# A hand-ordered four-layer graph kernel: a block sum written in place, six sum buffers, three attention tiles, eleven halves of x

## The chip, the core and the metric

The kernel runs on one core of a Trainium2 chip. A core has TensorE (PE in the profile: matmuls and transposes), VectorE (DVE), ScalarE (ACT), GpSimd (POOL) and SyncE (SP, which here issues the DMAs). Each works through its own queue in order and waits for others by semaphores. The time is the device time of one execution in microseconds, and less is better.

## The reference

The input x has 128 graphs of 128 nodes with 512 features, in fp32. All graphs share one 128x128 adjacency matrix. Four layers follow each other, each with a residual and a layer norm. The kernel receives all of them, and the second adds a per-row amount that the following layer norm takes away again, so that only its second normalisation is left of it (the kernel folds this into a factor of the first).

```python
# layer 0: x = LN(x + norm_adj @ (x @ W0) + bias), with norm_adj = D^-1/2 adj D^-1/2
# layer 1: x = LN(x + max over a row of relu(pre)), with the adjacency for both weights
# layer 2
q, k, v = x @ Wq.T, x @ Wk.T, x @ Wv.T
rel = adj.T * (q @ k.T)
x = LN(x + (rel / norm(rel, axis=2)) @ v)
# layer 3
h = x @ W3
e = leaky_relu(s1[:, None] + s2[None, :]) * adj      # s1 = h @ a1, s2 = h @ a2
x = LN(x + elu(softmax(e) @ h + beta * h))
```

## The kernel before

**Groups and steps.** Four graphs make a group, and there are 32 groups, 0 to 31. A group is a chain of 240 steps for the repeated part. Some of their names, in the order of one group's chain:

- `ld` loads a half of x (two graphs, 512 KB); `y` is norm_adj times x, transposed; `cy` copies it to SBUF; `bi` adds the bias to x on POOL.
- `w1` to `w7` are the seven products of one level of Strassen's scheme for y times W0; `dw` adds them onto x; `stw`, `gw`, `pow`, `apw` are layer norm statistics, guard, power and application.
- `xt` and `xd` transpose x: blocks of 32x32 on DVE (`xt`), and an exchange by 16 DMAs of 64 KB on SP (`xd`, line 680). The result is the tile that the profile calls x_<group>T.
- `z1` to `z7` and `v1` to `v7` are products of that transpose, with Wq and Wk folded into one weight `gq`, and with Wv. `c` copies or `d` adds bring them into C_z and C_v. `r` multiplies z with x (line 1142, tile pr), `rm`, `sq`, `rp` mask it and take its norm, `rt`, `wr`, `cr` transpose it through DRAM (relT), `f` multiplies it with v (line 1190, tile pl_v), and `fa` adds it onto x with a running total (line 1199).
- `mnv`, `qv`, `gv`, `pov`, `apv` normalise: negative mean and squares on ACT, the power on POOL (line 588), the application on ACT (line 1029).
- `nt` and `nd` transpose x once more (tile n_<group>T), again with 16 DMAs; `k1` to `k7` multiply it with W3 into C_k.
- `sc` are the two attention scores of a graph on DVE (line 1214); `pw` and `pe` send one of them through DRAM and back to all partitions; `pl`, `ej`, `ei`, `ex`, `rd`, `so` are leaky relu, mask, maximum, exponential and division; `at`, `aw`, `cat` transpose the result through DRAM (attT); `h` multiplies it with C_k (line 1190, tile pl_k); `em`, `ee`, `ea` finish the elu; `mnk`, `qk`, `gk`, `pok`, `apk` normalise, and `fin` stores.

**Two levels of Strassen.** A left side (y, x or n transposed) is a class `Left` with a tile of four blocks, `block(p, h)`, over halves of the graphs and halves of the features. `sum(0)` to `sum(3)` (steps `sy`, `sx`, `sn`) make its four sums on POOL; products 5, 6, 7 and 3 read them through `of`. `sum(i)` computes them in the order sum 0, 2, 1, 3; the one made second is `A(0,0) - A(1,0)`, read by product 7. Products 1, 2, 5 (for z and v also 4) are split once more: `l12`, `l5`, `l4` (method `small`) make POOL sums of 128x128 blocks; the first four small matmuls are the step `w1` (line 730), the further three have a name such as `w18`, and between them the steps `b` (ACT copies a part out of PSUM) and `e` (three DVE additions). Products that are not split have four matmuls of 256 columns (line 766).

**The order.** Each instruction's place in its engine's queue follows from three written strings. `HEAD` starts the first groups, `TURN` is repeated and moves every stage on by one group, and `TAIL` ends. A step is written as group.step, the group counted from the turn's base; text below uses true group numbers, as in 31.f1. Before, `TURN` is used 14 times. `BACK`, `FIRST` and `LAST` set which groups it spans. Group 31 has steps of its own (class attribute `HALVES`): it transposes its attention matrices on PE (prt, pat, ps2) in place of the way through DRAM, and its last products k and h are split into halves of the columns for one or two graphs.

**Buffers.** `Slotted.tile` takes the slot of a shared buffer from the strings of `SLOTS`, one character an allocation: `bank` (PSUM), `S` (the sums, 2 KB a partition, seven of them), `m` (attention tiles such as rel, ru, relT, e, s2, au, attT, 2 KB, four), `x` (halves of x, 4 KB, ten), `aT` (transposes, three) and others. A new tile in a slot waits for the last reader of the one before.

Of the kernel before, what the change touches and what calls it, by code (L numbers as in the profile page):

```python
# [37 lines left out]
F32 = mybir.dt.float32  # L38
# [10 lines left out]
        "012345012345013324015345231455124240510435012532245312312023543413421402402052145230142402"  # L49
        "405233100340153013205320521340135305355234252351453524503210430454115310512125312305211451"  # L50
        "412523102304253042541105305015021541030340351405232432352315320142424230314525325435403451"
        "025252541243050250302310324152525234530121521015041053425252503201454254142134120352525210"
        "514323523435403451025252541243050250302310324152525234530121521015041053425252503201454254"
        "142134120352525210514323523435403451025252541243050250302310324152525234530121521015041053"
        "425252503201454254142134120352525210514323523435403451025252541243050250302310324152525234"
        "530121521015041053425252503043201513105140152035033042453510140541524513202020314220445020"
        "545523405212550033235143024014515313210213142055015354151041043201425125523020130023054354"
        "2045151501250312315415401340132145131523152403145324501324051324051"
    ),
    "S": (  # L60
        "012345601326054321502461532143250123654012106425231064104632501462035142560413524651203546"
        "413406524103561463205164231534062135410216534012605403216504352651403256124320651423046145"
        "320641563062145360231534062135410216534012605403216504352651403256124320651423046145320641"
        "563062145360231534062135410216534012631450326154036413652014326504152602324316052432560324"
        "152630645016325064152306"
    ),
    "l1": (
        "010111010101010010101011001101001011010010110100101101001011010010110100101101001011010010"
        "110100110010110011010110100100110"
    ),  # L70
    "l2": (
        "010101010101010010110110110110110110110110110110110110110110110110110110110110110101110101"
        "01"
    ),
    "C": (
        "010101010101011010101011011011011011011011011011011011011011011011011011011011011011011010"
        "10101010"
    ),
    "aT": (
        "012100212102102012012102012102012102012102012102012102012102012102012102012102102012012010"  # L80
        "2110210"
    ),
    "m": (
        "012301202302301210320100130133212013131201310310213231201012103232120131323021213103232120"
        "131323021213103232120131323021213103232120131323021213103232120131323021213103232120131323"
        "02121310233221302022132020213201210312121203210030"
    ),
    "x": (
        "0123457869789012345768901234576890123457689012345768901234576981032"
    ),  # L90
    "q": (
        "010101010101010001001010101010101010101010101011010101010101010100101010101001010101010101"
        "010101010101010001010101010101010101010101010101010101010101010101010101010101010101010101"
        "010101010101010101010101010101010101010101010101010101010101010101010101010101010101010101"
        "010101010101010101010101010101010101010101010101010101010100010101010101010101010101010101"
        "01010101010101010101010101010101010101010101010101010101010101010101010"
# [3 lines left out]
MIDS = 4  # L100
SUMS = 7
# [5 lines left out]
LAST = -7  # L107
# [3 lines left out]
0.ld1 2.ld0 0.ld0 2.ld1 1.ld1 1.ld0 s.warm s.deg s.root s.nadj s.adjt s.nadjT 0.y10 0.y01 0.cy10  # L111
1.y10 0.cy01 1.y11 1.cy10 1.y01 1.cy11 0.y11 s.m012_0 1.cy01 3.ld1 s.s00 0.w2 s.m012_1 0.cy11
s.s02 0.bi10 s.m012_3 0.y00 0.bi01 2.y10 s.s01 0.cy00 2.y11 0.bi00 0.w1 s.m05_0 0.sy0 s.s03 2.y00
1.y00 0.bi11 s.m05_1 1.cy00 0.sy2 s.m012_2 0.w5 1.bi10 s.m05_3 0.sy3 0.dw1 s.m05_2 0.w6 0.sy1
0.dw2 s.sk0 1.ly12 s.sk2 s.g1 0.dw6 s.s30 0.w7 s.cg1 1.sy0 s.m312_0 1.bi11 0.dw7 s.m312_1 0.w4
1.bi00 0.dw5 s.bi 0.w3 s.sa1 2.cy10 0.dw4 2.cy00 s.sk1 2.cy11 s.g2 s.sa0 0.dw3 0.stw3 3.y11 1.bi01
0.stw0 s.g5 0.stw1 s.sa2 s.dg2 2.y01 s.s31 1.sy2 0.stw2 1.w2 2.cy01 s.s33 s.g6 0.gw s.sa3 1.bw2
s.m35_0 1.w1 s.cg6 0.pow 1.ew2 s.g7 1.bw1 s.m35_1 2.bi11 1.ew1 0.apw0 0.apw1 1.w28 0.xt0 1.ly5
1.w18 s.cg7 s.sk3 s.la 0.apw2 0.apw3 1.sy1 1.w5 1.dw1 3.ld0 0.xt2 s.g4 1.bw5 0.xt1 2.bi01 0.xt3
s.q11 1.w6 2.bi00 s.cg4 0.xd 1.ew5 s.mg12_0 3.bi11 1.w58 s.dg5 s.q02 s.g3 2.bi10 1.dw6 1.dw2 1.w7  # L120
s.dg3 2.ly12 s.mg12_1 1.dw7 s.mg12_3 1.w4 s.sg0 1.dw5 s.sg2 2.w2 s.sg1 4.ld0 2.w1 s.m312_3 2.bw2
s.sg3 2.ew2 2.bw1 0.z1 0.sx0 s.vt3 s.vt0 0.sx2 s.vt1 2.w28 0.cz1 1.dw4 1.sy3 s.vt2 0.z6 1.stw3
s.vd 0.sx1 1.stw2 1.w3 0.cz6 0.sx3 s.mg4_0 2.sy0 0.z5 2.ew1 1.dw3 2.sy1 0.z7 s.mg4_1 2.ly5 1.stw1
2.w18 s.mg4_3 0.cz7 0.z2 2.sy2 0.dz5 1.stw0 0.z4 0.dz2 1.gw s.mg5_0 s.mg12_2 1.pow s.mg5_2 0.z3
0.cz4 s.mg5_1 s.m35_3 1.apw3 s.mg5_3 3.y10 2.dw1 1.apw2 s.sv0 0.v1 1.apw0 3.bi10 2.dw2 1.apw1
1.xt2 s.sv1 0.v2 0.cv1 1.xt3 0.dz3 0.v6 1.xt0 0.dv2 1.xt1 0.r0 s.sv3 0.cv6 1.xd s.mv5_0 2.w5
s.mv4_0 s.mv5_1 s.mv4_1 s.sv2 0.r1 2.bw5 s.mv4_3 s.mv12_0 0.r2 2.ew5 0.r3 s.mv12_2 s.mv12_1 2.w58
s.mv5_3 s.mv12_3 0.rm 0.v7 s.q10 0.sq0 0.rt 0.sq1 2.w6 0.sq2 s.q12 0.cv7 s.q03 0.sq3 s.q00 0.rp
0.v4 s.q13 0.v5 3.cy11 s.q01 3.cy10 0.wr 2.dw6 0.cv4 4.ld1 3.sy0 s.wt0 s.s32 2.w7 2.sy3 0.cr 0.dv5
s.wt1 s.mv5_2 3.y00 1.sx0 2.dw7 0.v3 s.mg4_2 3.cy00 1.lx12 2.dw5 2.w4 s.mv4_2 0.dv3 0.f3 2.dw4  # L130
3.sy1 0.f1 2.stw2 0.f2 3.bi00 2.stw3 1.v1 0.fa3 1.lx4 0.fa2 1.z1 1.bv1 0.fa1 2.w3 1.bz1 1.ev1
1.lx5 1.ez1 0.f0 1.sx2 1.v5 2.dw3 0.fa0 1.z18 1.sx3 1.bv5 2.stw0 1.v18 0.mnv 1.cz1 1.ev5 1.z5
1.sx1 0.qv2 1.z6 2.stw1 0.qv1 1.cv1 0.qv0 1.z2 1.cz6 1.v6 1.bz2 0.qv3 1.ez2 1.bz5 1.z7 0.gv 2.gw
1.ez5 0.pov 1.cv6 2.pow 1.z28 0.apv3 1.z4 1.cz7 1.dz2 0.apv0 1.z58 0.nt3 2.apw0 1.v2 0.sc00 2.apw2
0.nt0 3.y01 1.bz4 0.sc01 0.apv2 1.v58 3.bi01 1.ez4 3.cy01 1.v7 0.apv1 0.nt2 3.ly5 2.apw1 0.sc10
1.bv2 1.z48 2.apw3 0.nt1 1.v4 1.cv7 3.ly12 1.dz4 0.nd 1.ev2 3.w5 1.bv4 1.dz5 1.v28 3.bw5 0.sc11
1.z3 3.ew5 1.dv2 3.w1 0.sc20 3.w2 1.dz3 3.bw1 0.sc21 3.w58 3.ew1 1.r0 1.r1 0.sc30 3.bw2 1.ev4 1.r2
1.r3 3.ew2 1.v48 0.sc31 3.w18 1.dv4 3.w28 0.pw 3.dw1 1.rm 0.k2 0.sn0 3.dw2 1.sq0 2.xt1 1.sq1 0.sn2
0.pe 2.xt0 0.k1 1.sq2 2.xt2 1.sq3 0.sn3 2.xt3 0.k5 1.rt 0.ck1 2.xd 1.rp 1.dv5 s.m312_2 0.sn1 0.pl3
0.dk2 1.v3 0.pl0 s.m35_2 0.pl1 0.pl2 3.sy2 0.k6 1.dv3 0.ej 3.w6 0.ck6 3.sy3 0.ei 0.ex0 0.k7 3.dw6  # L140
0.ex3 0.ex2 0.ex1 3.w7 0.rd 0.ck7 0.so0 0.dk5 0.so1 4.y11 3.dw7 1.wr 0.k4 3.dw5 4.bi11 0.at 0.aw
2.lx12 3.w4 4.cy11 1.cr 0.ck4 3.w3 3.dw4 2.sx0 3.stw2 0.cat 2.z1 3.stw3 2.sx2 2.z2 3.dw3 2.bz1
3.stw0 1.f2 2.sx1 2.bz2 3.stw1 2.v1 2.lx5 2.ez2 1.f0 3.gw 0.k3 1.fa2 2.bv1 3.pow 1.fa0 2.ez1 1.f1
2.lx4 3.apw0 0.dk3 1.f3 3.apw3 3.xt0 3.apw1 2.z18 1.fa1 3.apw2 0.h0 1.fa3 2.cz1 2.v5 3.xt2 1.mnv
3.xt1 0.h3 1.qv0 2.ev1 2.z28 1.qv1 2.z6 3.xt3 1.qv2 2.dz2 3.xd 1.qv3 0.em3 2.v18 0.em0 2.bv5 1.gv
0.h1 2.cz6 2.ev5 1.pov 0.ee0 2.z7 0.ee3 0.em1 1.apv3 0.ea0 1.apv0 0.ea3 2.v58 2.cz7 2.z5 1.sc00
0.ee1 1.apv1 4.y00 1.sc01 2.bz5 0.ea1 4.y10 1.apv2 4.bi00 2.ez5 4.cy00 4.y01 4.cy10 4.bi10 1.sc10
0.h2 4.cy01 1.sc11 2.z4 4.bi01 2.cv1 0.em2 2.v2 1.sc20 2.bz4 4.sy0 0.ee2 2.z58 2.ez4 2.bv2 2.v6
4.ly12 2.ev2 1.nt1 2.z48 2.cv6 1.sc21 2.v28 2.dz4 2.sx3 2.v7 1.sc30 3.sx0 2.dz5 4.w1 1.sc31 2.cv7
3.lx12 2.dv2 2.z3 1.pw 4.bw1 1.nt2 4.ew1 2.v4 2.dz3 1.pe 4.w18 3.sx2 1.nt0 2.bv4 2.r0 1.nt3 3.lx5  # L150
4.dw1 2.r1 2.ev4 3.z2 4.sy2 0.ea2 2.r2 1.pl3 1.pl0 2.r3 4.sy1 0.mnk 1.pl2 4.w6 1.pl1 3.sx1 2.rm
0.qk3 2.rt 2.sq0 1.ej 2.v48 0.qk2 2.wr 4.dw6 3.z1 2.dv4 1.nd 2.sq1 3.lx4 0.qk1 4.w7 1.ei 2.dv5
3.bz1 1.ex0 3.ez1 1.ex1 2.v3 1.ex3 4.sy3 1.ex2 4.dw7 2.sq2 3.bz2 1.rd 2.sq3 1.so0 3.z18 3.ez2
0.qk0 4.w4 3.sx3 3.cz1 2.dv3 0.gk 1.so1 3.z5 4.dw4 3.z6 0.pok 3.bz5 3.ez5 2.rp 0.apk3 3.z28 3.cz6
# [253 lines left out]
def kernel(  # L408
# [17 lines left out]
    P = 128  # L426
# [163 lines left out]
    class Left:  # L590
# [22 lines left out]
        def sum(self, i):  # L613

            A = self.block
# [792 lines left out]
```

## Time and profile before

| | us |
|---|---|
| median of 3 runs | 1981.98 (1981.17 to 1983.0) |
| the profiled execution, device time | 1983.26 |
| its span, first to last instruction | 1981.5 |
| granted TensorE clock, share of full | 0.998 |

The profile page gives busy time by engine, the span in 40 slices and the costliest groups of instructions. Other answers of the same trace are used below: sums by stretch, the chain of waits in order of time, the waits of one engine, and timelines. A group's row reads: line, engine, operation, output tile <- input tiles, shapes, count | busy us, mean ns of one | idle time before it and what ended it. Matmuls overlap one another, so their paces are taken from starts, not from their own lengths. An fp32 matmul of the program leaves two records.

```profile
L766 PE MATMUL p_w<-w,S_y 128*128 128x256 f32 x512 | 121.2, 379 | 0.4 <-DVE x L582 0.4
L1029 ACT ACTIVATE x<-x,nb,r 128x512 f32<-128x512 f32 x383 | 289.6, 808 | 28.8 <-POOL nb L585 28.5
L585 POOL TENSOR_TENSOR x<-x,bias_bc 128x512 f32<-128x512 f32 x128 | 165.7, 1299 | 122.0 <-PE py L935 92.3
```

PE's rows have almost no idle time before them, ACT's and POOL's have much.

### The profile page before, as it was taken

The numbers are of one execution on the slowest core, as the hardware profiler recorded it, in microseconds if no ns is written. First come the engines' busy times: TensorE is split into PE (matmuls) and PEld (weight loads), VectorE is DVE, ScalarE is ACT, GpSimd is POOL, SyncE is SP. The second block draws the span as 40 slices with busy tenths as digits, with TensorE's granted clock in tenths as the row PEclk, the third lists the DMA queues.
The fourth block names the chain that finished last, engine by engine and source line by source line (L and its number), as shares of the span: only waits on it lengthen the run. The fifth ranks groups of instructions, "written<-read, shape, count | busy, mean of one in ns | idle before, by whom it ended". The sixth has DMA issues, their size and how long they took to land.

```text
span 1981.5 us, 37439 instructions
## 1 busy us (share of the span) xinstructions
PE 1954.1 (99%) x12405; PEld 1723.5 (87%) x12405; DVE 1645.2 (83%) x3801; ACT 1125.0 (57%) x2800; POOL 1372.1 (69%) x1702
## 2 busy tenths in 40 slices
PE   8999999999999999999999999999999999999997
PEld 7888988888888988888988888988889888898885
DVE  7888787888788888888888888888888888787887
ACT  2245556565655656565556556556656556566467
POOL 7557678676687776786766776766877767777652
PEclk9999999999999999999999999999999999999999
DMA  5523455334444345444345443445343454434434
GB/s 199 85 52 66 96 80 135 60 87 101 106 100 95 66 89 107 104 99 76 81 91 113 98 106 58 92 98 112 92 102 59 92 106 100 96 62 107 76 73 107
DMA packets 737312, 184.55 MB, mean 93 GB/s; under 512 B 689376, under 2 KB 689760, under 8 KB 737120
## 3 DMA queue, kind: packets, MB, share of 16 engines
q1 hardware_dynamic: 736976, 182.03, 43.7%
q8 instruction: 100, 1.64, 0.4%
q14 instruction: 92, 0.75, 0.1%
q10 hardware_dynamic: 144, 0.13, 0.0%
HBM read 64.03 MB, written 49.87 MB: 57 GB/s over the span
## 4 chain that ended last, share of the span: by engine, by line
PE 86%; SPq 4%; POOL 3%; DMA 2%; DVE 2%; ACT 1%; issue 1%; POOLq 0%; DVEq 0%; ACTq 0%
PE p_w L766 10%; PE p_k L766 10%; PE p_v L730 9%; PE p_z L730 8%; PE p_v L766 8%; PE p_z L766 8%; PE p_w L730 7%; PE p_k L730 6%; PE pr L1142 5%; PE pl_k L1190 5%; PE pl_v L1190 5%; PE py L935 5%; SPq L680 4%; POOL x L585 1%; PE pk L1059 1%
## 5 line engine op out<-in xcount | busy, mean ns | idle before, releaser
L1029 ACT ACTIVATE x<-x,nb,r 128x512 f32<-128x512 f32 x383 | 289.6, 808 | 28.8 <-POOL nb L585 28.5
L585 POOL TENSOR_TENSOR x<-x,bias_bc 128x512 f32<-128x512 f32 x128 | 165.7, 1299 | 122.0 <-PE py L935 92.3
L588 POOL TENSOR_TENSOR r<-v,minus_half 128x4 f32<-128x4 f32 (+1 forms) x99 | 99.1, 1001 | 200.8 <-ACT v L1025 189.5
L582 DVE TENSOR_TENSOR x<-p_w,x 128x512 f32<-128x512 f32 x224 | 153.6, 686 | 48.4 <-PE p_w L766 22.3
L1214 DVE SCALAR_TENSOR_TENSOR e<-x,wa_bc 128x512 f32<-128x512 f32 x256 | 172.3, 673 | 1.4 <-ACT x L1029 0.7
L579 ACT COPY C_k<-p_k 128x512 f32<-128x512 f32 x124 | 71.7, 579 | 150.0 <-PE p_k L766 137.5
L935 PE MATMUL py<-nadjT,x 128*128 128x128 f32 x1024 | 134.8, 277 | 1.0 <-DVE x L1310 0.6
L935 PEld LDWEIGHTS py<-nadjT,x 128*128 128x128 f32 x1024 | 126.9, 193 | 5.1 <-issue 1.4
L1190 PE MATMUL pl_k<-C_k,attT 128*128 128x512 f32 x248 | 122.9, 594 | 1.8 <-DMA attT<-d_a 1.7
L1190 PE MATMUL pl_v<-C_v,relT 128*128 128x512 f32 x248 | 121.0, 593 | 0.9 <-DMA relT<-d_r 0.9
L766 PE MATMUL p_z<-S_x,gq 128*128 128x256 f32 x512 | 121.3, 380 | 0.2 <-DVE C_z L582 0.2
L766 PE MATMUL p_w<-w,S_y 128*128 128x256 f32 x512 | 121.2, 379 | 0.4 <-DVE x L582 0.4
L766 PE MATMUL p_v<-wvT,S_x 128*128 128x256 f32 x512 | 121.1, 379 | 0.0
L1305 ACT ACTIVATE pl_k<-pl_k 128x512 f32<-128x512 f32 x127 | 73.4, 581 | 80.3 <-DVE x L1302 79.4
L766 PE MATMUL p_k<-w,S_n 128*128 128x256 f32 x496 | 117.3, 379 | 0.0
L1199 DVE SCALAR_TENSOR_TENSOR x<-pl_v,r,x 128x512 f32<-128x512 f32 x128 | 94.7, 746 | 23.9 <-PE pl_v L1190 18.9
L582 DVE TENSOR_TENSOR p_z<-p_z,q_z 128x128 f32<-128x128 f32 x248 | 107.3, 433 | 8.5
L582 DVE TENSOR_TENSOR p_v<-p_v,q_v 128x128 f32<-128x128 f32 x248 | 107.3, 433 | 8.5
L766 PEld LDWEIGHTS p_z<-S_x,gq 128*128 128x128 f32 x512 | 94.2, 190 | 21.2 <-issue 6.9
L582 DVE TENSOR_TENSOR C_v<-p_v,C_v 128x512 f32<-128x512 f32 x127 | 86.5, 681 | 28.9 <-ACT C_v L579 13.5
L766 PEld LDWEIGHTS p_w<-w,S_y 128*128 128x128 f32 x512 | 93.2, 190 | 12.2 <-issue 1.1
L766 PEld LDWEIGHTS p_k<-w,S_n 128*128 128x128 f32 x496 | 91.6, 190 | 14.0 <-issue 2.9
(1627 smaller groups left out, 6246.6 us busy)
## 6 DMA issues: line engine op xcount, KB each, us to landing
x<-in_x_dram SPq DMA_DIRECT2D x64, 512.0 KB, 4.5
out_dram<-x SPq DMA_DIRECT2D x127, 256.0 KB, 2.5
d_r<-ru SPq DMA_DIRECT2D x31, 256.0 KB, 2.0
relT<-d_r SPq DMA_DIRECT2D x124, 64.0 KB, 2.5
s<-d_s SPq DMA_DIRECT2D x31, 256.0 KB, 3.8
d_a<-au SPq DMA_DIRECT2D x31, 256.0 KB, 2.3
attT<-d_a SPq DMA_DIRECT2D x124, 64.0 KB, 4.0
w<-in_L_gnn_weight_dram SPq DMA_DIRECT2D x1, 1024.0 KB, 9.5
```

The source lines that it names most:

```text
L582: nc.vector.tensor_tensor(o, a, b, f)
L585: nc.gpsimd.tensor_tensor(o, a, b, f)
L588: nc.gpsimd.tensor_tensor(o, v, minus_half[:, : v.shape[-1]], ALU.pow)
L680: nc.sync.dma_start(out=o[rows(to), :, :, rows(q)], in_=self.u[rows(q), :, :, to])
L730: nc.tensor.matmul(self.banks[i][:, r, bass.ts(c, P)], lhsT=lhsT, rhs=rhs, start=(not then and n == 0), stop=(n == len(steps) - 1), skip_g ...
L766: nc.tensor.matmul(ps[:, j, :], lhsT=lhsT, rhs=rhs, start=(i not in ONTO and j == 0 and kc == 0), stop=(j == 1 and kc == 1), skip_group_ch ...
L935: nc.tensor.matmul(o, lhsT=self.x_chunk(b, kc), rhs=nadjT, start=True, stop=True)
L1029: nc.scalar.activation(xt, xt, AF.Identity, bias=self.nb[k][:, b : b + 1], scale=self.rstd[k][:, b : b + 1],)
L1142: nc.tensor.matmul(self.pr[:, b, :], lhsT=self.whole["z"][:, fc, b // 2, bass.ts(b % 2, P)], rhs=self.xT.chunk(b, fc), start=(fc == 0), st ...
L1190: nc.tensor.matmul(ps, lhsT=left[:, b, :], rhs=self.whole[k][:, b, :], start=True, stop=True)
L1199: nc.vector.scalar_tensor_tensor(xt, self.pf[b], self.rnorm[:, b : b + 1], xt, ALU.mult, ALU.add, accum_out=self.total("v", b),)
L1214: nc.vector.scalar_tensor_tensor(wide(self.e), self.x(b), 1.0, wide(wa_bc[k]), ALU.mult, ALU.mult, accum_out=self.s[:, k, b : b + 1],)
```

## The change

The second sum that `Left.sum` makes gets no buffer of its own for y and n: it is written over block (1,0) of the transposes, of which it is itself a reader. For x it keeps its buffer. The memory that this frees, with one attention tile less, goes to an eleventh half of x: 2 + 2 KB against 4 KB a partition. The three order strings and all slot strings are written anew for these buffers; `TURN` is used 13 times in place of 14, `TAIL` being one group longer (`LAST`).

```diff
-MIDS = 4
-SUMS = 7
+MIDS = 3
+SUMS = 6
...
-LAST = -7
+LAST = -8
...
-    xp = Slotted(ctx.enter_context(tc.tile_pool(name="xp", bufs=10)))
+    xp = Slotted(ctx.enter_context(tc.tile_pool(name="xp", bufs=11)))
...
             n = (0, 2, 1, 3)[i]
-            self.s[n] = big.tile([P, 2, 2, P], F32, tag="S", name=f"S{n}_{self.name}", bufs=SUMS)
+            if i == 1 and self.name[0] != "x":
+                self.s[n] = A(1, 0)
+            else:
+                self.s[n] = big.tile([P, 2, 2, P], F32, tag="S", name=f"S{n}_{self.name}", bufs=SUMS)
```

The order strings hold the same 7733 steps before and after, each once. Two stretches of them, with true group numbers, that the prediction speaks of. First the PE steps from the last `f` of group 31 to the first step that reads n_31T (other engines' steps left out):

```
before: 31.f0 29.k5 29.k6 29.k28 30.k1 29.k58 30.k5 29.k7 30.k18 30.k2 29.k4 29.k3 30.k6
        29.h3 29.h2 30.k7 30.k28 30.k58 30.k4 29.h0 30.k3 29.h1 31.pe 31.k3
after:  31.f1 29.h2 30.k1 30.k5 30.k2 29.h3 30.k18 30.k58 29.k3 30.k6 30.k28 29.h0 29.h1
        30.k7 30.k4 30.k3 31.pe 31.k0
```

POOL's steps that lie between n_30T and 31.pov:

```
before: 30.sn0 30.ln12 30.ln5 30.sn2 30.sn3 31.pov
after:  30.sn0 30.ln12 30.ln5 30.sn2 30.sn1 30.sn3 29.sn3 31.pov
```

And the DVE steps of the opening up to 0.dw6 (s. marks the preparation of weights):

```
before: s.s00 s.m012_1 s.s02 s.m012_3 s.s01 s.m05_0 s.s03 s.m05_1 s.m012_2 s.m05_3 0.dw1
        s.m05_2 0.dw2 s.sk0 s.sk2 0.dw6
after:  s.s00 s.m012_1 s.s02 s.m012_3 s.m05_0 s.s01 s.m05_1 s.s03 0.dw1 s.m012_2 s.m05_3
        0.dw2 s.m05_2 s.sk0 0.dw6
```

## The prediction

> **What bounds the kernel now.** I read the page's busy rows first, then one stretch of the repeated turn, then the chain in order of time for the pace of TensorE's rows, and last the ending.
>
> ```profile
> PE 1954.1 (99%) x12405; PEld 1723.5 (87%) x12405; DVE 1645.2 (83%) x3801; ACT 1125.0 (57%) x2800; POOL 1372.1 (69%) x1702
> PE   8999999999999999999999999999999999999997
> ```
>
> TensorE (PE) is idle for 1981.5 - 1954.1 = 27.4 us, and only the first and last slices are below 9. By stretches of the trace, 10.6 us of that lie before 240 us, 3.6 between 240 and 1740, 13.2 after. No other engine is above 83%.
>
> ```profile
> 900.00:960.00 60.00, 60.00 (x389) 53.28 (x389) 50.65 (x118) 35.22 (x88) 43.22 (x54) 1.00 0.44 93
> ```
>
> The columns are length, then PE, weight loads, DVE, ACT, POOL busy, granted clock, DMA share, GB/s. In the middle PE is busy for all 60 us at full clock.
>
> ```profile
> 156.85 1.73 PE p_k L766 x8
> 221.12 2.58 PE pl_v L1190 x6
> 855.81 2.68 PE pr L1142 x24
> 866.12 1.79 PE p_w L730 x16
> 915.88 2.68 PE pr L1142 x24
> ```
>
> Start, length, what, from the chain in order of time. One fp32 matmul leaves two records, so a matmul over 256 columns takes 1.73/4 = 0.433 us, over 512 2.58/3 = 0.86, over 128 1.79/8 = 0.224. A group has 56, 8 and 130 of them: 24.3 + 6.9 + 29.1 = 60.2 us. The turn repeats every 915.88 - 855.81 = 60.07 us: no wait is left in it, and no order can make it shorter.
>
> [...] The paces decide, since the turn's period equals them.
>
> **The change, part by part.** [...] Only waits can change, and what lies before the first and behind the last matmul.
>
> *Third sum in place.* `sum(1)` still is one POOL operation (128x512, about 1.25 us), now written over block (1,0), whose other reader, sum 0, precedes it on the same queue. Product 7 then reads the transposes' tile; product 4, which reads it anyway, comes after 7 in the turn for w and k alike, so the tile is freed no later. Cost 0. The x transposes keep their copy, as `pr` reads that block.
>
> *Six sum buffers, three attention tiles.* Fewer buffers can make a writer wait for a reader. I put the new turn's steps beside PE's order with the rows' durations, as an estimate: the tightest consumer is `pl_v_0` behind DVE's addition into C_v, with 0.24 us to spare; in the old turn the tightest has 0.58. Positive, so 0; if it is short by the same 0.24, 13 turns cost 3.1 us. Below 0 it cannot go.
>
> *Eleven halves of x.* The turn fetches half a group further ahead. The row gives 4.5 us to landing, and in the turn shown the two loads are issued at 941.7 and first read by y at 963.6, so 0: hidden before and after.
>
> *Opening.* PE waits before 240 us sum to 10.6, of which about 4.5 lie before the first y product, whose steps stay.
>
> ```profile
> PE p_w L766 <- DVE x L582: 3.8, 4, 1.7
> PE p_z L766 <- DMA x_0T<-sq_x: 1.2, 1, 1.2
> ```
>
> The new order moves two DVE weight sums (1.5 and 1.35 us) behind 0.dw1, which frees product 0.w6 about 2.7 us sooner. But they then stand before 0.dw2 and 0.dw6, so 0.w7 gains 0.7. Against it, 0.z1 has 1.7 us less PE work ahead of it (the z1 that waited 1.2 for x_0T), and three loads of x are issued before x_0T. I take 0; bounds -6.1 (all these waits go) and +3.
>
> *Middle and the two changeovers.* The 3.6 us there (waits for attT, n_3T) may go, or the new buffers may cost as much: 0, bounds -3.6 and +3.6.
>
> *Ending.* This is where the order loses cover. Old order, one fence for each engine's timeline:
>
> ```profile
> 1919.56 3.60 PE L1190 MATMUL pl_v<-C_v,relT_end 128*128 128x512 f32 x8
> ...
> 1948.47 3.69 PE L1059 MATMUL pk<-w,n_31T 128*128 128x256 f32 x16 [0.30 <-DVE x L1302]
> ```
> ```profile
> 1922.04 1.27 POOL L585 TENSOR_TENSOR S_n<-n_30T 128x512 f32<-128x512 f32 x1 [1.63 <-DMA n_30T<-sq_n]
> ...
> 1930.52 1.02 POOL L588 TENSOR_TENSOR r<-v,minus_half 128x4 f32<-128x4 f32 x1
> ```
> ```profile
> 1935.88 10.70 SPq L680 DMA_DIRECT2D n_31T<-sq_n  x16
> ```
>
> From the end of pl_v (1923.1) the last group goes through sums, squares, `pov` on POOL, normalisation, transposes and SP's 16 DMAs; the first is issued at 1935.88, 12.8 us later, the last at 1946.0 and landed 2.1 later, at 1948.1. So 25.0 us from pl_v to n_31T. PE had 25.1 us of other work in between: the chain just fitted.
>
> In the new order, 31.f1 (the last pl_v) is followed by 30.k1, k5, k2 (4 small matmuls each, 2.7), their second parts (2.0), four products of 30.k and 29.k3 (8.7), four pl_k (3.4), four transposes (0.9), and then 31.k0, which reads n_31T: 17.7 us. Missing are 29.k5, k6, k28, k58, k7, k4 (0.9 + 1.73 + 0.67 + 0.67 + 1.73 + 1.73 = 7.4), done earlier. Lower end: 25.0 - 17.7 = 7.3 us of wait.
>
> But POOL's queue makes it later. The last 30.f is now 25.4 us of PE before 30.k1 (37 before). The same 25.0 brings n_30T; the rows above give 4.2 us more to the l tile of k1 and 5.9 to that of k5, so k5 waits 25.0 + 5.9 - 26.5 = 4.4 us. Then POOL has four sums of 1.24 before 31.pov (two before): pov starts 25.0 + 5.9 + 5.0 = 35.9 us after 30.f's end. In the row, 5.4 pass from pov to the first DMA and 12.2 from that to the last landing: 53.5. PE's own work from 30.f's end to 31.k0 is 42.3. Wait: 53.5 - 42.3 = 11.2 us, with the 4.4 inside it. I take 11.2; upper end 15, if DVE's queue delays 31.f too.
>
> [...] SP issues one each 0.63 to 0.67 us.
>
> *Behind the last matmul.* It starts at 1969.21, and 11.7 us pass from its end to the span's. The new order ends with one full 31.h1 in place of an h2 and two halves; the softmax steps of group 31 run while PE waits. The shortest chain (max, exp, min, statistics, power, shift, apply, DMA) is about 8.2 us by the rows: bounds 0 and -3.5; I take -2.
>
> **Sum.** 0 + 0 + 11.2 - 2 = +9.2 us. The profiled execution's own time is 1983.26 (span 1981.5), so 1992.5; against the median 1981.98, 1991.2.
>
> **Rivals.**
> - *Slower further, 2003 (chance 0.12).* The 0.24 us in the turn is not there, and each of 13 turns waits about 0.9 us, as a `p` in C_v is late: 1991.2 + 12. For it: DVE at 84% of the turn. Against: the old turn with 0.58 has no wait at all.
> - *No change, 1982 (0.13).* The opening gives back what the ending costs: -6.1 - 3 + 9.2 = 0. For it: the DVE waits around p_w. Against: 0.w7 gains only 0.7.
> - *Faster, 1976 (0.05).* One mechanism: the waits of opening and middle vanish, -9.7. It decides once the ending costs under 5.7; at the ending's lower bound (7.3 - 3.5 = 3.8) 1981.98 - 9.7 + 3.8 = 1976. Against: x_0T and the weights land no sooner.
> - *It doesn't do what it says.* If the in-place block held the transposes' tile, y's copies would wait; product 4 behind 7 excludes that.
>
> **Numbers.** The forecast (0.70) has its own range from 1987 (lower ends of the ending) to 1997. Together with no change at 1982 and part of the slower rival: 1982.5 to 1999. A measurement can tell about 0.2% (4 us) from no change. Faster 0.05, same 0.13, slower 0.82.
>
> **What would show it.** The turn still 60.07 us; idle PE before 240 us near 10.6; in the last 60 us waits of `p_k` for POOL's l_n, then of pk_None for n_31T, 11 us together; a last matmul followed by under 11 us. I am wrong if 31.k0 starts without a wait, or if the turn's period has grown.

## The result, and the profile after

| | before | after |
|---|---|---|
| median, us | 1981.64 (1981.17 to 1983.0) | 2004.66 (2003.05 to 2006.52) |
| the profiled execution, device time | 1983.26 | 2005.17 |
| its span | 1981.5 | 2003.0 |
| granted TensorE clock | 0.998 | 0.996 |

The kernel is slower by a ratio of 1.0115, interval 1.0099 to 1.0131: about 23 us where the forecast had 9.2, and outside the range. (Before's median is now that of four runs.) Lines of the changed kernel lie 17 to 20 further down: the product lines L730, L766, L1142 and L1190 are L750, L786, L1162 and L1210, the helpers L582, L579 and L585 are L599, L596 and L602.

From the page of after: the busy rows, PE's row of 40 slices, and the row that answers to ACT's application of a norm.

```profile
PE 1962.8 (98%) x12405; PEld 1725.9 (86%) x12405; DVE 1634.7 (82%) x3801; ACT 1132.5 (57%) x2800; POOL 1367.9 (68%) x1702
...
PE   8999999999999999999999999999999999999987
...
L1049 ACT ACTIVATE x<-x,nb,r 128x512 f32<-128x512 f32 x383 | 286.6, 806 | 59.2 <-POOL nb L602 58.5
```

The counts are the same: no work was added. PE's busy time grew by 8.7 us without one more instruction (half clock, below, is some 5 of them); its idle time grew from 27.4 to 40.2 us. ACT's longer wait for POOL, 28.8 us before, is that of an engine with slack.

The turn first, in a stretch of after and in the same links of the chain of waits, two turns one after the other:

```profile
900.00:960.00 60.00, 60.00 (x389) 53.09 (x388) 49.35 (x118) 35.57 (x88) 42.92 (x54) 1.00 0.45 93
```
```profile
862.15 1.78 PE pr L1162 x16
...
922.23 1.78 PE pr L1162 x16
```

922.23 - 862.15 = 60.08 us, as before. So I looked for the time in PE's starts: the difference from one start to the next, less the pace of a record (0.112, 0.2165 and 0.4295 us for 128, 256 and 512 columns), is time lost at that place.

| stretch of the span, us | lost before | lost after | difference |
|---|---|---|---|
| 0 to 80 | 13.4 | 18.7 | +5.3 |
| 80 to 540 | 6.3 | 4.9 | -1.4 |
| 540 to 1840 | -2.0 | 2.0 | +4.0 |
| 1840 to the last start | 2.5 | 19.0 | +16.5 |
| behind the end of the last matmul | 11.7 | 8.9 | -2.8 |

The sum is +21.6, within rounding the difference of the spans. (A small negative value comes from the paces, which are rounded.) Of the +16.5, 5.5 lie between 1860 us and the end of the last `f` of group 31 (1943.4 us, before 1923.2), and 11.5 behind it; a wait of before at 1853 takes 0.5 off. Of the +4.0, 2.6 lie between 1500 and 1740, in `TAIL`.

Each column is one execution. Six of the kernels below (all with after's steps as far as about 1400 us) tell how firm the upper rows are: they lose 15.5 to 18.6 us before 80 us and 5.6 to 9.7 between 80 and 540. So after's +5.3 is at the upper end of what its opening costs and its -1.4 at the lower end of the next stretch. The two together are +2.0 to +6.5 in those six, and near +4 in after.

### The profile page after: what moved, and what is told of

It reads as the page before. It is cut to its first block, busy times and chain, and to the rows that moved or that the text cites. A ratio compares the mean times of both kernels' runs of the same rounds, so it can differ in the third digit from the quotient of the medians.

```text
span 2003.0 us, 37436 instructions
## 1 busy us (share of the span) xinstructions
PE 1962.8 (98%) x12405; PEld 1725.9 (86%) x12405; DVE 1634.7 (82%) x3801; ACT 1132.5 (57%) x2800; POOL 1367.9 (68%) x1702
## 4 chain that ended last, share of the span: by engine, by line
PE 80%; POOL 6%; DVE 4%; SPq 4%; DMA 2%; ACT 2%; issue 1%; POOLq 0%; ACTq 0%; DVEq 0%
PE p_w L786 9%; PE p_k L786 9%; PE p_v L750 8%; PE p_z L750 8%; PE p_z L786 8%; PE p_v L786 7%; PE p_w L750 6%; PE p_k L750 5%; PE pr L1162 5%; PE pl_k L1210 5%; PE py L955 4%; PE pl_v L1210 4%; SPq L700 4%; POOL l_x L602 1%; POOL l_n L602 1%
## 5 line engine op out<-in xcount | busy, mean ns | idle before, releaser
L599 DVE TENSOR_TENSOR x<-p_w,x 128x512 f32<-128x512 f32 x224 | 153.1, 687 | 86.2 <-PE p_w L786 72.6
L602 POOL TENSOR_TENSOR x<-x,bias_bc 128x512 f32<-128x512 f32 x128 | 164.8, 1295 | 61.5 <-PE py L955 61.0
L596 ACT COPY C_k<-p_k 128x512 f32<-128x512 f32 x124 | 71.5, 576 | 99.4 <-PE p_k L786 90.0
L1210 PE MATMUL pl_k<-C_k,attT 128*128 128x512 f32 x248 | 124.2, 594 | 2.3 <-DMA attT<-d_a 1.8
L786 PE MATMUL p_v<-wvT,S_x 128*128 128x256 f32 x512 | 121.3, 380 | 0.9 <-ACT C_v L596 0.9
L786 PE MATMUL p_z<-S_x,gq 128*128 128x256 f32 x512 | 121.3, 380 | 0.9 <-ACT C_z L596 0.7
L1210 PE MATMUL pl_v<-C_v,relT 128*128 128x512 f32 x248 | 120.2, 594 | 1.6 <-DMA relT<-d_r 0.9
L599 DVE TENSOR_TENSOR p_z<-p_z,q_z 128x128 f32<-128x128 f32 x248 | 107.4, 433 | 8.5
L599 DVE TENSOR_TENSOR p_v<-p_v,q_v 128x128 f32<-128x128 f32 x248 | 107.4, 433 | 8.5
L596 ACT COPY C_z<-p_z 128x512 f32<-128x512 f32 x97 | 56.5, 583 | 94.0 <-PE p_z L786 85.8
L786 PEld LDWEIGHTS p_z<-S_x,gq 128*128 128x128 f32 x512 | 93.2, 190 | 14.3 <-issue 2.5
L786 PEld LDWEIGHTS p_v<-wvT,S_x 128*128 128x128 f32 x512 | 92.8, 190 | 12.8 <-issue 1.2
L599 DVE TENSOR_TENSOR C_z<-p_z,C_z 128x512 f32<-128x512 f32 x127 | 86.8, 684 | 15.6 <-ACT C_z L596 8.4
L596 ACT COPY C_v<-p_v 128x512 f32<-128x512 f32 x97 | 56.6, 583 | 71.9 <-PE p_v L786 40.0
L1322 DVE SCALAR_TENSOR_TENSOR x<-pl_k,x 128x512 f32<-128x512 f32 x127 | 85.1, 684 | 12.9 <-PE pl_k L1210 12.7
L599 DVE TENSOR_TENSOR C_v<-p_v,C_v 128x512 f32<-128x512 f32 x127 | 86.2, 680 | 11.3 <-PE p_v L750 4.8
```

The lines of the kernel that those rows point to most:

```text
L596: nc.scalar.copy(o, i)
L599: nc.vector.tensor_tensor(o, a, b, f)
L602: nc.gpsimd.tensor_tensor(o, a, b, f)
L786: nc.tensor.matmul(ps[:, j, :], lhsT=lhsT, rhs=rhs, start=(i not in ONTO and j == 0 and kc == 0), stop=(j == 1 and kc == 1), skip_group_ch ...
L1210: nc.tensor.matmul(ps, lhsT=left[:, b, :], rhs=self.whole[k][:, b, :], start=True, stop=True)
```

## The opening, in the trace

PE's timeline of after, the products that waited:

```profile
25.44 3.57 PE L786 MATMUL p_w<-w_t,S_y 128*128 128x256 f32 x8 [2.88 <-DVE x L599]
...
34.57 2.91 PE L786 MATMUL p_w<-w_t,y_0T 128*128 128x256 f32 x8 [2.10 <-DVE x L599]
```

The first is 0.w6; this is the row of before:

```profile
25.45 1.96 PE L766 MATMUL p_w<-w_t,S_y 128*128 128x256 f32 x8 [1.74 <-DVE x L582]
```

Two things are to be seen. Its wait for 0.dw1 is 2.88 us where it was 1.74: it starts no sooner than before, although two sums had been moved out of 0.dw1's way, and PE comes to it earlier. And its eight records take 3.57 us where the same eight take 1.99 elsewhere. The windows of after (length, then PE, weight loads, DVE, ACT, POOL busy, granted clock, DMA share, GB/s) say why:

```profile
22.50:25.26 2.76, 0.06 (x1) 0.00 (x0) 2.76 (x3) 0.00 (x0) 2.76 (x3) 1.00 1.05 388
25.26:28.67 3.41, 3.23 (x8) 2.61 (x9) 3.13 (x6) 0.00 (x0) 3.33 (x5) 0.50 1.06 388
...
35.50:38.91 3.41, 3.41 (x9) 2.71 (x9) 3.41 (x5) 1.31 (x3) 3.41 (x3) 0.50 0.00 0
...
1970.85:1974.27 3.42, 3.42 (x5) 1.33 (x4) 0.69 (x1) 3.27 (x8) 0.75 (x1) 0.50 0.51 133
```

Behind three of its waits TensorE ran at half clock for 3.41 us each, and each such stretch cost about 1.7 us (half of 3.41; 0.w6 took 3.57 - 1.99 = 1.6 longer). That makes 5 of the 24 us lost ahead of the last matmul.

The wait itself is DVE's. Its timeline of after, then that of before:

```profile
12.56 1.23 DVE L548 TENSOR_TENSOR m<-w 128x256 f32<-128x256 f32 x1 [7.01 <-DMA w<-in_L_gnn_weight_dram]
13.72 0.68 DVE L532 TENSOR_TENSOR w_t<-w 128x512 f32<-128x512 f32 x1
14.32 1.48 DVE L548 TENSOR_TENSOR m<-w,m 128x256 f32<-128x256 f32 x1
15.73 1.75 DVE L532 TENSOR_TENSOR w<-w 128x512 f32<-128x512 f32 x1
...
24.71 0.68 DVE L599 TENSOR_TENSOR x<-p_w,x 128x512 f32<-128x512 f32 x1
```
```profile
12.75 0.42 DVE L531 TENSOR_TENSOR m<-w 128x256 f32<-128x256 f32 x1 [6.97 <-DMA w<-in_L_gnn_weight_dram]
13.09 0.68 DVE L515 TENSOR_TENSOR w_t<-w 128x512 f32<-128x512 f32 x1
13.69 0.42 DVE L531 TENSOR_TENSOR m<-w,m 128x256 f32<-128x256 f32 x1
14.03 0.68 DVE L515 TENSOR_TENSOR w<-w 128x512 f32<-128x512 f32 x1
...
21.95 1.49 DVE L531 TENSOR_TENSOR w<-w 128x256 f32<-128x256 f32 x1
23.35 1.35 DVE L531 TENSOR_TENSOR m<-w_t,m 128x128 f32<-128x128 f32 x1
24.62 0.68 DVE L582 TENSOR_TENSOR x<-p_w,x 128x512 f32<-128x512 f32 x1
```

The last row of each is 0.dw1: 24.71 against 24.62. The two sums that left the queue, in before the two rows above it, had taken 1.49 + 1.35 = 2.84 us. Three of the four first sums now take 0.81, 1.06 and 1.07 more, 2.94 together. What stands beside them is POOL:

```profile
12.25 1.26 POOL L602 TENSOR_TENSOR y_0T<-y_0T 128x512 f32<-128x512 f32 x1 [2.82 <-ACT y_0T L596]
13.74 3.19 POOL L602 TENSOR_TENSOR x<-x,bias_bc 128x512 f32<-128x512 f32 x2 [0.23 <-DMA bias_bc<-in_L_gnn_bias_dram]
```

The first is 0.sy1, the in-place sum, which the new order puts before 0.bi; in before POOL was idle until 14.07. From 14.32 to 24.7 us in after, a sum of DVE among POOL's sums of 128x512 takes some 1.07 us more in each of three sizes: 0.28 became 1.35 for 128x128, 0.42 became 1.49 for 128x256, 0.68 became 1.75 for 128x512. (Among POOL's shorter sums of 128x256 it takes less: 0.81 for 128x128 at 25.64 us in after. Later sums of 128x512, as at 34.44, take 1.15.) POOL's two sums from 13.74 us on take 1.6 each where the one before them took 1.26, and 0.dw1, which reads one operand from PSUM, takes 0.68 in both kernels. What in the chip makes the two engines lengthen each other's sums is not shown.

## The ending, in the trace

PE's timeline of after, the waits in order of time:

```profile
1909.21 1.99 PE L786 MATMUL p_z<-S_x,gq 128*128 128x256 f32 x8 [0.68 <-ACT C_z L596]
1911.88 1.98 PE L1210 MATMUL pl_v<-C_v,relT 128*128 128x512 f32 x4 [0.68 <-ACT C_z L596]
...
1928.32 1.99 PE L786 MATMUL p_v<-wvT,S_x 128*128 128x256 f32 x8 [0.93 <-ACT C_v L596]
...
1939.71 3.70 PE L1210 MATMUL pl_v<-C_v,relT_end 128*128 128x512 f32 x8 [0.50 <-ACT relT_end L596]
...
1945.25 1.10 PE L1210 MATMUL pl_k<-C_k,attT 128*128 128x512 f32 x2 [1.83 <-DMA attT<-d_a]
...
1950.67 0.46 PE L750 MATMUL p_k<-w,n_30T 128*128 128x128 f32 x2 [0.79 <-DVE p_k L599]
...
1962.53 1.99 PE L786 MATMUL p_k<-w_t,n_30T 128*128 128x256 f32 x8 [2.26 <-ACT C_k L596]
...
1968.19 0.32 PE L1153 MATMUL ps<-ident,s 128*128 128x128 f32 x1 [1.61 <-DVE e L1234]
1969.97 5.37 PE L1079 MATMUL pk_None<-w,n_31T 128*128 128x512 f32 x8 [1.46 <-DMA n_31T<-sq_n]
```

1939.71 is the last `f`. Behind it there is no one long wait but five of 0.8 to 2.3 us, ended by DMA, DVE, ACT, DVE and DMA, and the last is followed by half clock (5.37 us for records that take 3.60). Before it, around 1900 to 1930, many waits below 1 us add up. Why 29.h2 (1945.25) waits is in SP's queue of after (start, length):

```profile
1928.89 10.71 SPq L700 DMA_DIRECT2D n_30T<-sq_n  x16
1939.70 0.57 SPq L1247 DMA_DIRECT2D d_s<-s  x1
1940.31 2.60 SPq L727 DMA_DIRECT2D attT<-d_a  x4
```

The four DMAs that bring attT of group 29 back are queued behind the 16 issues of n_30T; 29.h2 is now the first step behind the last `f`; before, twelve steps stood ahead of the first `h` of group 29.

## The experiments

Theory 1 was that the time is lost through the order, most of it in the ending, the rest in the opening. Its rivals were the smaller buffers themselves, the in-place sum, and particular waits of the ending. In the diffs of order strings below only one engine's steps are shown, with true group numbers, where nothing else is said.

**The old order of the ending.** The changed kernel with the 2276 steps of `TAIL` in their old order; head, turn and in-place sum stay as changed. That order holds up to seven sums and four attention tiles at a time, so one of each is lent from a half of x that is not in use there; this run gives back order and buffers together, the next one buffers alone.

```diff
+                if (tag, SLOTS[tag][n]) in (("S", "6"), ("m", "3")):
+                    t = host()
...
+            spare.append(xp.pool.tile([P, 2, D], F32, tag="x_9", name="spare", bufs=1))
...
-31.f1 29.h2 30.k1 30.k5 30.k2 29.h3 30.k18 30.k58 29.k3 30.k6
+31.f2 31.f1 31.f3 31.f0 29.k5 29.k6 29.k28 30.k1 29.k58 30.k5 29.k7 30.k18
```

> HEAD, TURN, the in-place sums and the buffers stay as changed; only the steps of TAIL (2276 of 7733, from about 1430 us on) stand in the old kernel's order. That order holds up to seven sums and four attention tiles at once, so the eleventh half of x, which it does not need there, lends room for one of each. Theory 1, the extra time is in the order of the ending: from 1500 us on PE's starts lose 21.4 us against their paces in the changed kernel and 1.8 in the old one, so 19.6 us go and the time is 1985 (1983 to 1988). Theory 2, the in-place sums and fewer buffers make the waits themselves: within 3 us of 2004.7.

1989.8 us, ratio 1.0034 [1.0021, 1.0047]. From 1500 us on PE lost nothing over its paces (21.4 in after). Its row of slices, which ends in 87 in after:

```profile
PE   8999999999999999999999999999999999999997
```

15 of the 23 us are the ending's; some 7 remain. In the trace they lie in the opening (3.3), between 80 and 540 us (2.7) and between 540 and 1840 (3.4, half of it where the two orders join), less 2.4 in the last stretch.

**Buffers in place of order.** The new order, with one more sum and one more attention tile lent from about 1800 us on.

```diff
-        "02121120122110120200102211202101002012122201111202"
...
+        "10220021020221201100201122101320232130230231010123"
```

> The changed kernel's order, untouched; but once the last half of x is loaded (about 1800 us) a free half of x lends room for a seventh sum and a fourth attention tile, and the slots of TAIL are dealt anew, each tile taking the one that has been free longest. Theory 1 (order): no buffer is waited for, so 2003 to 2006.5. Theory 2 (the ending waits because a writer waits for a buffer's last reader): at least 5 us less, 1999 or below.

2006.67, ratio 1.0117 [1.0101, 1.0132]: no gain, so these buffers are not what the ending waits for. The order is what remains: the old one needs the buffers that the change took away, so another had to be written.

**The in-place sum alone**, put into the old kernel. Where an in-place sum would come before sum 0, which still reads that block, it is put behind it (all engines' steps are shown, the group counted from the turn's base). (In the preparation of Wq it is written before its other reader, so values of gq differ there.)

```diff
-3.bv5 5.sy1 4.xt1 3.r0 1.ee1 1.em3 5.sy0 3.r1
+3.bv5 4.xt1 3.r0 1.ee1 1.em3 5.sy0 5.sy1 3.r1
...
+            if i == 1 and self.name[0] != "x":
+                self.s[n] = A(1, 0)
```

> The old kernel with the in-place sum alone (seven sum buffers, four attention tiles, ten halves kept; four third sums moved behind the first sum that reads the same block). Theory 1: the in-place write costs nothing, 1981 to 1983.5. Theory 2: the block stays occupied until product 7 and its writers wait, 0.2 us or more in each of 32 groups, so 1988 or more.

1984.01, ratio 1.0003 [0.9994, 1.0012]. It costs nothing that can be measured.

**How much of the ending.** Two cuts of the first experiment: only the 523 steps behind 31.w3 in the old order, and only the 216 steps behind 31.f1.

```diff
-31.f1 29.h2 30.k1 30.k5 30.k2 29.h3 30.k18 30.k58 29.k3 30.k6
+31.f1 30.k1 30.k5 30.k18 30.k2 29.k3 30.k6 29.h3 29.h2 30.k7 30.k28
```

> The changed kernel, with only the steps behind 31.w3 (523, from about 1857 us) in the old kernel's order; a free half of x lends a fourth attention tile, which that order holds for moments, and a seventh sum buffer. Theory 1, these last 145 us alone hold the ending's loss: PE's starts lose 19.0 us against their paces behind 1840 us in the changed kernel and 2.5 in the old one, so 16.5 us go and the time is 1988 (1985.5 to 1991). Theory 2, the loss comes from what the order before that point left late (x_31T, n_29T): less than 8 us go.

1991.34, ratio 1.0048 [1.0033, 1.0063]: 13.3 us less than after. The last products in PE's timeline of this kernel:

```profile
1923.56 1.89 PE L803 MATMUL p_v<-wvT,S_x 128*128 128x256 f32 x8
...
1927.07 3.60 PE L1227 MATMUL pl_v<-C_v,relT_end 128*128 128x512 f32 x8
1930.50 0.39 PE L767 MATMUL p_k<-w_t,S_n 128*128 128x128 f32 x2
...
1955.56 3.69 PE L1096 MATMUL pk<-w,n_31T 128*128 128x256 f32 x16 [0.28 <-DVE x L1339]
```

24.9 us from the end of pl_v to the product that reads n_31T (25.3 in before), filled with work, and a wait of 0.28: the old cover is back.

> The changed kernel, with only the steps behind 31.f1 (216, the stretch whose wait the prediction summed) in the old kernel's order, in which 31.pov stands before 29.sn3 and 30.sn1. Theory 1, the cover is gone before that point: PE has 17.7 us of work left in any order against the 25.0 from pl_v to n_31T, so under 3 us go, 2002 or above. Theory 2, the prediction's: POOL's sums before 31.pov make 3.9 of the 11.2 us, so 4 us or more go, 2000.5 or below.

2001.54, ratio 1.0103 [1.0088, 1.0118]: between the two theories. In its timeline 30.k1 and 30.k5 do wait for POOL's l_n, as the prediction had it for the new order:

```profile
1942.11 0.71 PE L767 MATMUL p_k<-m,l_n 128*128 128x128 f32 x4 [1.13 <-POOL l_n L619]
...
1944.15 0.71 PE L767 MATMUL p_k<-m,l_n 128*128 128x128 f32 x4 [0.89 <-POOL l_n L619]
...
1949.73 3.26 PE L803 MATMUL p_k<-w,S_n 128*128 128x256 f32 x8 [1.93 <-POOL S_n L619]
```

This order is good only together with what stood before it: in the old kernel n_30T was there earlier. So the loss cannot be put right behind the last `f` alone. 13.3 - 3.1, some 10 us, come with the steps between 31.w3 and 31.f1, some of them as waits behind 31.f1. (The runs of last_f spread over 6 us, so the 3.1 is rough.)

**POOL's queue before 31.pov.** The power moved ahead of three sums.

```diff
-30.sn0 30.ln12 30.ln5 30.sn2 30.sn1 30.sn3 29.sn3 31.pov
+30.sn0 30.ln12 30.ln5 30.sn2 31.pov 30.sn1 30.sn3 29.sn3
```

> The changed kernel with one POOL step moved: 31.pov before 30.sn1, 30.sn3 and 29.sn3, so that it starts as soon as 31.gv is done. In the changed kernel 26.6 us pass from the end of the last 31.f to the start of 31.k0, and 31.pov stands 3.9 us behind 31.gv. Theory 1, DVE takes the normalised rows up no sooner, since 30.ek2 is in its queue until 1953.4: 0.9 us less, 25.7, and the time 2002.5 to 2005. Theory 2, the prediction's: POOL's detour is on the path that ends last: 3.6 to 3.9 us less, 23 or under, and the time 2000 to 2001.5.

2006.03, ratio 1.0122 [1.0108, 1.0136]. From the end of 31.f1 to 31.k0 it is 27.1 us, 26.6 in after. POOL's timeline of this kernel, and what PE then waits for:

```profile
1951.42 1.02 POOL L605 TENSOR_TENSOR r<-v,minus_half 128x4 f32<-128x4 f32 x1
...
1955.13 1.27 POOL L602 TENSOR_TENSOR S_n<-n_29T,S_n 128x512 f32<-128x512 f32 x1
```
```profile
1956.45 1.99 PE L786 MATMUL p_k<-w,S_n 128*128 128x256 f32 x8 [0.81 <-POOL S_n L602]
...
1966.36 1.99 PE L786 MATMUL p_k<-w_t,n_30T 128*128 128x256 f32 x8 [2.08 <-ACT C_k L596]
```

The power starts 5.1 us after the last `f` has ended where it took 8.7, and nothing ends sooner: the first DMA of n_31T is issued 14.7 us after the last `f`, in after 14.1. 29.k3 waits for 29.sn3, and 30.k4 waits as before for an ACT copy that stands behind the exponentials of group 30.

**The chain of 30.rt.** In after 30.rt starts 23.7 us after 30.rm has ended (1902.32, 1878.59), in before 0.5. Here 30.rt, 30.wr, 30.cr and the products 30.f are moved ahead, with a fourth attention tile lent. (30.f there reads v before 30.dv3 has added its last part.)

```diff
-8.ck1 10.rm 8.k58 10.bv4 9.sc30 8.k28
+8.ck1 10.rm 10.rt 10.wr 8.k58 10.bv4 9.sc30 8.k28
...
-8.dk5 8.k4 9.nt2 11.sx0 9.nt1 9.nt3 11.sx1 8.k3 9.nt0
+8.dk5 8.k4 10.cr 9.nt2 11.sx0 9.nt1
+9.nt3 11.sx1 8.k3 10.f3 10.f2 10.fa3 10.f0 10.fa2 10.f1 10.fa0 10.fa1 9.nt0
```

(Numbers as in the string: 10 stands for group 30. All engines' steps are shown.)

> The changed kernel, with the steps of group 30 that wait for the third attention tile (30.rt, 30.wr, 30.cr, and the four 30.f and 30.fa) moved ahead: 30.rt directly behind 30.rm instead of 24 us later behind 28.qk1, the four 30.f between 28.k3 and 28.h2. A fourth attention tile for it is lent by a free half of x. Theory 1, it matters only as cover: the split products of group 31 still stand in one block and DVE's additions for them still come late, so the waits from 31.v18 to 31.f0 (6.5 us in the changed kernel) stay between 5 and 8 us, and the time 2001.5 to 2007. Theory 2, the late 30.rt is itself the cost: 3 us or more of these waits go, 2001 or below.

2014.52, ratio 1.0165 [1.015, 1.0181], worse than either theory had it. PE lost 13.2 us from 1880 to 1943, 6.8 in after: 30.f waits 2.03 for relT, and later products of z wait 2.04 and 2.29. As 30.f was moved too, this shows only that starting the chain earlier in this way does not win the time back; what a late 30.rt costs by itself stays open.

**The opening.** DVE's opening of the changed kernel laid anew: the large sums first, the small ones between the `dw`, ten preparations of W3 put off to about 100 us.

```diff
-s.m012_0 s.s00 s.m012_1 s.s02 s.m012_3 s.m05_0 s.s01 s.m05_1 s.s03 0.dw1 s.m012_2 s.m05_3 0.dw2
+s.s00 s.s02 s.s01 s.s03 s.m012_0 s.m012_1 0.dw1 s.m012_3 0.dw2 s.m012_2 0.dw6 s.sk0 s.m05_0 0.dw7
```

> The changed kernel with DVE's opening alone in another order: the four sums of the first weight that 0.w5, 0.w7, 0.w6 and 0.w4 read come first, the sums for the small products behind them between the 0.dw, and ten preparations of the last weight wait until about 100 us. Theory 1, DVE's queue beside POOL is what PE waits for in the opening, and the two waits of 2.9 and 2.1 us bring two half-clock windows: 0.w4 starts near 29 in place of 34.57 us, no half clock before 100 us, and the time falls by 6 to 9 us, to 1996 to 1999. Theory 2, DMA landings or the bias on POOL end those waits: less than 2 us.

The trace does what theory 1 says of DVE's queue: 0.dw1 at 20.90, and the opening loses 14.3 in place of 18.7. The time doesn't: 2007.2 (2002.3 to 2012.0), ratio 1.0119 [1.0097, 1.0141]. The profiled execution had a span of 2000.2 and a mean clock of 0.998; the three others, 3 to 10 us slower, had 0.995 or 0.996; where in them the clock was lower is not on record.

Only 0.sy1 moved, behind the four 0.bi:

```diff
-0.sy1 0.bi11 0.bi10 0.sy2 0.bi00 0.bi01
+0.bi11 0.bi10 0.sy2 0.bi00 0.bi01 0.sy1
```

> The changed kernel with one POOL step of the opening moved: 0.sy1, the third sum of y written in place, stands behind the four 0.bi instead of before them. In the changed kernel it runs from 12.2 to 13.5 us, beside DVE's first weight sum, which takes 1.23 us there and 0.42 us in the old kernel. Theory 1, DVE's weight sums are stretched by POOL's work beside them: that first sum takes 0.42 to 0.6 us again, 0.dw1 starts 0.8 to 1.2 us sooner than 24.7, and 0.w6 with it (24.2 to 24.6 in place of 25.44). Theory 2, DVE's queue is set by the landing of the weight alone: 0.w6 within 0.3 us of 25.44. The whole time cannot tell the two apart: 2001 to 2006 by either.

DVE's timeline of this kernel:

```profile
12.55 0.42 DVE L548 TENSOR_TENSOR m<-w 128x256 f32<-128x256 f32 x1 [6.67 <-DMA w<-in_L_gnn_weight_dram]
...
13.49 0.42 DVE L548 TENSOR_TENSOR m<-w,m 128x256 f32<-128x256 f32 x1
13.83 1.76 DVE L532 TENSOR_TENSOR w<-w 128x512 f32<-128x512 f32 x1
...
22.83 0.67 DVE L599 TENSOR_TENSOR x<-p_w,x 128x512 f32<-128x512 f32 x1
```

With POOL idle from 11.48 to 13.74 the first sums of 128x256 take 0.42 again; 0.dw1 comes 1.9 us sooner and 0.w6 waits 0.32. This shows the stretching. The total, 2004.8 (ratio 1.0119), is that of after: the waits come back later (1.76 and 2.42 us).

The old kernel with such an opening:

```diff
-s.m012_0 s.s00 s.m012_1 s.s02 s.m012_3 s.s01 s.m05_0 s.s03 s.m05_1 s.m012_2 s.m05_3 0.dw1
+s.s00 s.s02 s.s01 s.s03 s.m012_0 0.dw1 s.m012_1 0.dw2 s.m012_3 0.dw6 s.m012_2
```

> The old kernel, with DVE's opening alone in another order: the four sums of the first weight that 0.w5, 0.w7, 0.w6 and 0.w4 read come first, the sums for the small products go between the 0.dw, and ten preparations of the last weight wait until about 100 us. Theory 1, as in the changed kernel DVE's queue is what PE waits for: 0.w4 starts at 29 to 30 in place of 32.34 us, and 2 to 3.5 us go: 1978 to 1980, faster than both kernels. Theory 2, the waits come back at 0.z1 (x_0T) or at 0.f3 behind the postponed sums: less than 1 us, 1981 to 1983.

1985.43, ratio 1.0014 [1.0005, 1.0023]. The product 0.w4 starts 2.3 us sooner (30.07 against 32.34), and this is lost again: 2.4 us between 80 and 130, where the sums put off stand beside POOL (one took 1.48 us), and more behind that. No version tried beats the old kernel.

Old ending together with the first 400 steps in the old order:

> As tail_old, and the first 400 steps (to about 120 us) in the old kernel's order too; the third sum of Wq stays behind its first. What is left of the change: the in-place sums, six sums and three attention tiles outside TAIL, eleven halves of x, and the new order between 120 and 1430 us. Theory 1, opening and ending hold the whole difference: 1982 to 1986. Theory 2, the rest costs as much as tail_old still shows above the old kernel: 1988 or more.

1987.56, ratio 1.0034 [1.0021, 1.0047], between the theories. In the trace the opening is the old one (13.5 us lost, 16.7 in the run with the old ending alone), and the spans of the two profiled executions differ by 2.9 us. The medians, each against before's, do not show it: 5.9 us above before, 6.6 there, each within about 2.6. What remains lies between 80 and 540 us, where both lose more than before (9.6 and 9.0, before 6.3), and at the joint with `TAIL` (1.54 lost at one product). So the opening's loss is shown in traces, not in a time.

**The half clock.** Transposes of the identity, whose results nobody reads, put into the longest waits: before 0.w6, 0.w4, 1.w7 and 0.z1, in 29.h2, before the last score transposes and pk_None.

```diff
+        def fill(self, *n):
+            for _ in range(int("".join(map(str, n)))):
+                nc.tensor.transpose(wa_bc[0][:, 0, :], ident, ident)
...
+            for _ in range(11 if (b, h) == (0, None) else 0):
+                nc.tensor.transpose(self.pk[b, h][:, :P], ident, ident)
```

> The changed kernel with idle work on PE in its longest waits: 24 transposes of a constant before 0.w6, 17 before 0.w4, 12 before 1.w7, 17 before 0.z1, 14 before 29.h2, 12 in 31.pe, 11 before 31.k0, each to be overwritten; 0.11 us each at full clock, so no longer than the wait. Theory 1, a wait of 2 us or more on PE brings 3.41 us of half clock, 1.7 us each: no half-clock stretch at these places, mean clock 0.997 to 0.998, 3 to 5 us less, 2000 to 2001.5. Theory 2, the half clock has another cause, or the added work delays PE as much: mean clock 0.996, 2003 to 2008.

2002.05 (2000.43 to 2005.07), ratio 1.0105 [1.0088, 1.0121], the clock 0.998. The stretch from 1970.85 to 1974.27, in after at a granted clock of 0.50, has 1.00 here:

```profile
1970.85:1974.27 3.42, 3.42 (x15) 2.49 (x14) 0.77 (x4) 2.96 (x11) 0.00 (x0) 1.00 0.66 141
```

PE's waits of this kernel, in total, times, longest:

```profile
PE p_k L786 <- ACT C_k L596: 4.4, 4, 2.5
PE p_w L786 <- DVE x L599: 1.3, 3, 0.5
```

The first holds the wait of 30.k4, which was left unfilled; of the second, the filled waits of the opening, no more than 0.5 is left at a time. All four executions had a mean clock of 0.998, those of after 0.996 or 0.997: so the clock was higher here with work that only keeps TensorE busy. The median is 2.6 us lower than after's, less than expected, and the two kernels' runs overlap: a gain in time is not clear of the scatter.

## Why the prediction was right and wrong

The table's differences sum to 21.6 us where the forecast had 9.2. Of the 12.4 between, 5.3 are the opening's, 2.6 the middle's and 5.3 the ending's, less 0.8 behind the last matmul. Three steps failed: the opening was put at nothing, the ending was begun at the last `f`, and a wait was priced as the wait alone.

- *Turn, in-place sum, six sums and three tiles, eleven halves: 0.* Right. The turn takes 60.08 us; the in-place sum alone measured 1.0003; lending buffers back in the ending gave nothing.
- *Middle and changeovers: 0 within 3.6.* In after -1.4 and +4.0 make +2.6, inside the bounds. Other executions of the same steps lose more between 80 and 540 us, so that this term was too small in some of them. It does not come from a buffer that was waited for: a good part are waits in `TAIL`, such as one of 25.k6 for a copy (1.33).
- *"Opening. I take 0", upper bound +3.* This step failed: +5.3 in after, 2.1 to 5.2 in the six others. It counted the two sums that leave 0.dw1's queue and took the durations of the others as they were. 0.sy1, whose new place it did not look at, stretched them by what was gained: with it moved back, 0.dw1 came 1.9 us sooner. And it priced a longer wait as the wait alone: 3.4 of the 5.3 are half clock behind two waits. The bound from above came from the waits of before, and did not contain either.
- *"Ending": 11.2, from pl_v to n_31T.* The term has two parts. The missing cover, 7.3, was right. The rest, 3.9 us by which POOL's queue was to delay 31.pov and with it n_31T, failed: from the end of the last `f` to 31.k0 26.6 us pass, in before 25.3, so 1.3. PE lost 8.7 us more there than before. 30.k5 did not wait 4.4 us for POOL's l_n: 29.h2, now ahead of it, had waited 1.83 for attT, and the sums ended as they were needed. The detour of 31.pov was not on the path, since the experiment that removes it gains nothing; in its place stand waits of 0.8 to 2.3 us for SP's, DVE's and ACT's queues. Half clock behind the last of them (1.8) and waits among the last products (1.0) bring what is lost behind the last `f` to 11.5. So the size agrees by chance.
- *The same step, where it begins.* "This is where the order loses cover" was read as the last `f` alone. 5.5 us more are lost between 1860 us and its end: the new order has the fourteen steps of seven split products of 31.z and 31.v in one block (1892.9 to 1906.3), and DVE, which makes three additions for each product, had no pause over 0.3 us from 1890.6 to 1905.3. This last is read from the trace; no run isolates it, and the one try at a single chain in that stretch made it worse. That the stretch matters is shown: from 31.w3 on the old order gives 13.3 us back, from 31.f1 on only 3.1.
- *Behind the last matmul: -2.* Nearly right: -2.8.
- *The rivals.* The slower one named 2003, close to what was measured, but by a wait in each turn, and the turn's period is kept: its figure is luck. The faster one and the one of no change fall by the opening, which cost and gave nothing back.
- *The signs.* Neither sign of being wrong came: 31.k0 waits, and the turn's period has not grown. Idle time of PE before 240 us did tell, 13.2 us where 10.6 was named.
- *The paces, and SP's row.* The paces of PE's starts found each of the 21 us; the share of weight loads, 87% before and 86% after, hardly moved with them. SP's row for the 16 DMAs held: those of n_30T again took 10.71 us to issue.

## What to carry to other kernels

Where an order written by hand is exchanged for one that fits fewer buffers, compare the two orders stage by stage from the first product that moved, not only around the last one: a chain that just fitted before is lost in many waits of 1 to 2 us, and no single wait names it. The durations of DVE and POOL were those of their neighbours here (one 128x256 sum of DVE took 0.42 us beside an idle POOL and 1.23 beside 0.sy1), so a moved POOL step is priced on DVE's queue too. Waits of TensorE of 2.88 us, of 2.10, and of 1.61 with 1.46 close behind it were each followed by half clock in after, about 1.7 us more than the wait; price that too.

## What was not expected of the hardware

The half clock came, ahead of the last matmul of after, in three stretches of 3.41 us at a granted clock of 0.50, from 25.26, 35.50 and 1970.85 us on. In the 3.41 us before each of them (21.84 to 25.25, 32.08 to 35.49, 1967.44 to 1970.85) PE was busy for 0.72, 1.31 and 1.20 us, so idle for 2.69, 2.10 and 2.21. The length of one wait does not tell: the third stretch stands behind waits of 1.61 and 1.46 us, while 30.k4's 2.26, longer than 0.w4's 2.10, has none behind it in after: from 38.92 to 1970.80 the granted clock is 1.00. What halves the clock is not shown. After and its variants scatter more than before, and their slowest runs often have the lowest mean clock (0.995 in after_open's 2012.0, 0.998 in its 2002.3); no trace shows those runs, so the cause is not shown.

The other was the 1.07 us by which a DVE sum of the weights was longer among POOL's sums of 128x512 from 14.32 to 24.7 us in after, the same for 0.28, 0.42 and 0.68 us.
